# Bias rows turned on TensorE, unsummed last weights in two elements' denominators, and a piece of the MLP moved

## The chip, the cores and the metric

The kernel runs on one core of a Trainium2 chip. The metric is the device time of one execution, in microseconds; the kernel before takes 3774.46 us (median of three runs, 3773.48 to 3776.23). Lines L… are those of the kernel before unless the text says otherwise. Engines: PE is TensorE (matrix products), PEld its weight loads, DVE VectorE, ACT ScalarE, POOL GpSimd, SP the engine that issues most transfers. All data are 32-bit floats; in the trace each fp32 product shows as two passes (two MATMUL records).

## The reference

Sixteen batch elements, each an image of 256 channels by 1024 positions, go through two layers:

```python
# layer 0, per element; xs is (1024 positions, 256 channels)
qkv = (xs @ w_proj + b_proj)                 # 4 heads of 64, q k v each
attn = softmax(q @ k.T * 64 ** -0.5)
x = (attn @ v) @ w_out + b_out + xs
# layer 1
x = x + attention(group_norm(x, gn1_w, gn1_b), qkv_w, proj_w, proj_b, phys_bias)
#       8 heads of 32; phys_bias is one number per head, added before the softmax
h = group_norm(x, gn2_w, gn2_b)              # 32 groups
x = x + mlp_w2 @ gelu(mlp_w1 @ h + mlp_b1) + mlp_b2      # 256 -> 1024 -> 256
```

## The kernel before, in words

**Stages.** Each element passes attention 0 (`attention_a`, names ending in `_a`), group norm g, attention 1 (`attention_b`, names in `_b`), group norm h and the MLP (`m`). The query positions are handled in two blocks of 512 (index t), the channels in two halves of 128 (index c or co). The MLP of one element and the q, k, v products of the next fill TensorE while attention 1 waits for exponentials. Element 0 has no MLP before it, and element 15 no products after it, so these two have less to fill with.

**Attention.** Scores are computed with keys on the partitions: for each item (t, c) and each block of 128 keys, small TensorE products write scores to PSUM banks (L336, L468), ScalarE takes the exponential into an `e` tile (L344, L483), TensorE multiplies by v into an accumulator (L357, L519), and VectorE adds the `e` tiles up (L369, L498). In attention 1 a unit is two key blocks: block 0 and block 1, each with two `e` tiles of 128x1024. The function `add` is called for block 0 before the product with v of the unit before it, and for block 1 after it. The accumulator is one bank, 0, and is emptied after each unit, first by a copy on ScalarE (L530) and then by additions on VectorE (L532); the next score products use the same bank. At the end of an item the denominators are taken from the sums by products with `eones` (L541; four heads, one in each quarter of 32 columns of the array) into bank 1, copied out by ScalarE (L315), sent through DRAM to be spread over the partitions, inverted and multiplied in (L566). Small products use part of the array: "64*64" or "32*64" or "128*32" in the profile is rows by columns of one tile, and tiles on different parts run side by side.

**Tiles that change.** A setting `cols` decides whether `product` (L276 to L279) issues a 128-column product whole or as four of 32 columns. It is 32 or D inside the attentions and 128 at their ends. The function `out_proj` looks at the same setting to decide whether its two halves go to separate banks and are emptied one after the other (`apart`). At the end of attention 0, `first_half` of query block 0 (`o`, L429 to L434) runs with `cols` at 128, with the denominators `den_a` (L388) between its two halves.

**Start.** The weights `wp` arrive in six transfers from two queues (L92). The q and k copies out of PSUM add the bias `bqk` (L715), which `load_rest` fetches by six transfers of single 4-byte elements, four on ScalarE's queue behind `pb` (L143) and two on SP's (L145). `eones`, made from `pb` (L168 to L170), waits for ScalarE's exponential.

**End.** In the last element, five pieces of element 14's MLP are run inside attention 1 (`outputs[:5]`, L925) and the rest after it, where group norm h otherwise has TensorE wait; there `keep_warm` issues products whose results nobody uses. The kernel also keeps sums of denominators and of their inverses, and at its end checks that they lie in range (L959 to L970: sums, one turn on TensorE named `ok_row`, a minimum, a copy); a register is loaded from the result (L188), and a branch (L189) skips a second, general computation. These checks are written last in the program but stand between the warm products in the order of the engines, at 3708. The order within each engine's queue is set by a scheduler, with the order of the program as its start; lines inside `keep_in_program_order` are held.

Of the kernel before, what the change touches and what calls it, by code (L numbers as in the profile page):

```python
# [14 lines left out]
P = 128  # L15
# [38 lines left out]
@with_exitstack  # L54
def kernel(
    ctx: ExitStack,
    tc: tile.TileContext,
    x: bass.AP,
    w_proj: bass.AP,
    b_proj: bass.AP,  # L60
    w_out: bass.AP,
    b_out: bass.AP,
    gn1_w: bass.AP,
    gn1_b: bass.AP,
    gn2_w: bass.AP,
    gn2_b: bass.AP,
    qkv_wT: bass.AP,
    proj_wT: bass.AP,
    proj_b: bass.AP,
    phys_bias: bass.AP,  # L70
    mlp_w1T: bass.AP,
    mlp_b1: bass.AP,
    mlp_w2T: bass.AP,
    mlp_b2: bass.AP,
    out: bass.AP,
):
    nc = tc.nc
    B, C, S = x.shape
    HID = mlp_w1T.shape[1]
    CC = C // P  # L80
    SB = S // P
    NT = S // TB
    HC = HID // P
    GSZ = C // GROUPS

    const = ctx.enter_context(tc.tile_pool(name="const", bufs=1))


    wp = const.tile([P, CC, 3, HEADS0, D0], F32, name="wp")
    for t in (1, 0, 2):  # L90
        for cc in range(CC):
            (nc.gpsimd if cc else nc.scalar).dma_start(  # L92
                wp[:, cc, t],
                w_proj[cc * P : (cc + 1) * P, :].rearrange(
                    "p (h t d) -> p t h d", t=3, d=D0
                )[:, t],
            )


    bqk = const.tile([P, 3, HEADS0 // 2], F32, name="bqk")  # L100
    pb = const.tile([P, HEADS1], F32, name="pb")

    ident = const.tile([P, P], F32, name="ident")
    make_identity(nc, ident)
    mhalf = const.tile([P, CC], F32, name="mhalf")
    nc.gpsimd.memset(mhalf, -0.5)
    ones = const.tile([P, D0], F32, name="ones")
    nc.gpsimd.memset(ones, 1.0)

    def load_vec(v, n, name):  # L110
        t = const.tile([P, n], F32, name=name)
        nc.gpsimd.dma_start(t, v.rearrange("(c p) -> p c", p=P))
        return t

    bo = load_vec(b_out, CC, "bo")
    g1w = load_vec(gn1_w, CC, "g1w")
    g1b = load_vec(gn1_b, CC, "g1b")
    g2w = load_vec(gn2_w, CC, "g2w")
    g2b = load_vec(gn2_b, CC, "g2b")
    pjb = load_vec(proj_b, CC, "pjb")  # L120
    m1b = load_vec(mlp_b1, HC, "m1b")
    m2b = load_vec(mlp_b2, CC, "m2b")

    def load_mat(w, name):
        k, n = w.shape
        t = const.tile([P, k // P, n], F32, name=name)
        weights.append((t, w.rearrange("(c p) n -> p c n", p=P)))
        return t

    weights = []  # L130
    wo = load_mat(w_out, "wo")
    wq = load_mat(qkv_wT, "wq")
    wpj = load_mat(proj_wT, "wpj")
    w1 = load_mat(mlp_w1T, "w1")
    w2 = load_mat(mlp_w2T, "w2")


    def load_rest():
        bp = b_proj.rearrange("(g i t d) -> i t d g", i=2, t=3, d=D0)
        nc.scalar.dma_start(pb, phys_bias.partition_broadcast(P))  # L140
        for t in (1, 0):
            for i in range(2):
                nc.scalar.dma_start(bqk[i * D0 : (i + 1) * D0, t, :], bp[i, t])  # L143
        for i in range(2):
            nc.sync.dma_start(bqk[i * D0 : (i + 1) * D0, 2, :], bp[i, 2])  # L145
        for t, w in weights:
            nc.sync.dma_start(t, w)


    gind = const.tile([P, P // GSZ], F32, name="gind")  # L150
    nc.vector.tensor_reduce(
        gind, ident.rearrange("p (g j) -> p g j", j=GSZ), AX.X, ALU.add
    )
    gavg = const.tile([P, P // GSZ, GSZ], F32, name="gavg")
    nc.vector.tensor_scalar(
        gavg,
        gind.unsqueeze(2).to_broadcast([P, P // GSZ, GSZ]),
        1.0 / GSZ,
        None,
        ALU.mult,  # L160
    )
    gavg = gavg.rearrange("p g j -> p (g j)")


    ebias = const.tile([P, HEADS1], F32, name="ebias")
    eones = const.tile([P, HEADS1, D1], F32, name="eones")

    def exp_bias():  # L168
        nc.scalar.activation(ebias, pb, AF.Exp)
        nc.vector.tensor_copy(eones, ebias.unsqueeze(2).to_broadcast([P, HEADS1, D1]))  # L170

    bvo = const.tile([P, CC], F32, name="bvo")

    in_range = const.tile([P, 1], I32, name="in_range")

    with ExitStack() as first:
        first_pass(
            first, tc, x, out,
            dict(
                wp=wp, bqk=bqk, pb=pb, bo=bo, g1w=g1w, g1b=g1b, g2w=g2w,  # L180
                g2b=g2b, pjb=pjb, m1b=m1b, m2b=m2b, wo=wo, wq=wq, wpj=wpj, w1=w1,
                w2=w2, ident=ident, gavg=gavg, mhalf=mhalf, ones=ones, eones=eones,
                bvo=bvo, load_rest=load_rest, exp_bias=exp_bias,
                in_range=in_range,
            ),
        )

    good = nc.values_load(in_range[0:1, 0:1], min_val=0, max_val=1)  # L188
    with tc.If(good == 0):  # L189
        with ExitStack() as again:  # L190
            general_pass(
                again, tc, x, out,
                dict(
                    wp=wp, bqk=bqk, pb=pb, bo=bo, g1w=g1w, g1b=g1b, g2w=g2w,
                    g2b=g2b, pjb=pjb, m1b=m1b, m2b=m2b, wo=wo, wq=wq, wpj=wpj, w1=w1,
                    w2=w2, ident=ident, gavg=gavg, mhalf=mhalf, b_proj=b_proj,
                ),
            )


def first_pass(ctx, tc, x, out, k):
# [120 lines left out]
    def attention_a(b, qT, kT, v, project):  # L322
# [102 lines left out]
        while pending:  # L425
            weigh(*pending.pop(0))
            if not pending:


                cols[0] = P  # L430
                first_half = project(0, res)
                first_half((0,))
                yield
                first_half((1,))  # L434
                break
            yield

# [6 lines left out]
    def attention_b(b, qT, kT, v, project):  # L444
# [41 lines left out]

        def add(i, kb, es, block):
            if kb == 0 and block == 0:  # L490
                sums[i] = [
                    work.tile([P, 2, TB], F32, tag="es", name=f"es_{key}_{i}_{n}", bufs=4)
                    for n in range(G // 2)
                ]
                return
            for n in range(G // 2):
                d = sums[i][n]
                ins = nc.vector.tensor_add(d, es[n] if kb == 0 else d, es[2 * block + n])  # L498
                if block:
                    tc.keep_in_program_order(ins)  # L500
# [35 lines left out]
        def normalise(i, r, last):  # L536
            t, c = items[i]
            at_end = last and b == B - 1
            den = bank(f"den_{key}_{i}", 1)
            for g in range(G):  # L540
                nc.tensor.matmul(  # L541
                    den[g * D : (g + 1) * D, :],
                    k["eones"][:, c * G + g],
                    sums[i][g // 2][:, g % 2, :],
                    start=True,
                    stop=True,
                )
            if at_end:

                full = work.tile([P, CC * TB], F32, tag="full", name="rd_end", bufs=1)  # L550
                nc.vector.reciprocal(full[:, :TB], den)
                scale(i, r, last, full[:, :TB])
                for tot, what in ((dsum, den), (isum, full[:, :TB])):
                    part = small.tile([P, 1], F32, tag="part", name="part")
                    nc.vector.tensor_reduce(part, what, AX.X, ALU.add)
                    nc.gpsimd.tensor_add(tot[:, :1], tot[:, :1], part)
                return
            denominators(
                f"{key}_{i}", den_copy(f"{key}_{i}", den), TB,
                (3, 5) if last else (1, 1),  # L560
                lambda full: scale(i, r, last, full),
            )
# [32 lines left out]
    def out_proj(key, w, src, bias, xs, t, stats, then):  # L595
        todo = list(range(CC))

        def issue(cos=range(CC)):
            apart = cols[0] == P
            if not apart:  # L600
                both = wide(f"{key}_{t}")
            ps = {}
# [193 lines left out]
    def mlp(b, xb, hn):  # L796
# [16 lines left out]
        def reduce(t, co, half):  # L813
# [11 lines left out]
            nc.vector.scalar_tensor_tensor(  # L825
                y, ps, k["m2b"][:, co : co + 1], y, ALU.add, ALU.add
            )
            if half:
                nc.sync.dma_start(
                    out[b, co * P : (co + 1) * P, t * TB : (t + 1) * TB],  # L830
                    xb[:, co, t * TB : (t + 1) * TB],
                )

        return (
            [lambda t=t, hc=hc: hidden(t, hc) for t in range(NT) for hc in range(HC)],
# [29 lines left out]
    keep_warm(nothing, 3)  # L865
    xs = {0: load_x(0)}
    k["load_rest"]()
    tiles0, (first_qk, first_v) = qkv_0(0, xs[0])

    run_pieces(first_qk[::2] + first_qk[1::2] + first_v)  # L870
    k["exp_bias"]()


# [16 lines left out]
    for b in range(B):  # L890
# [31 lines left out]
            first = []  # L922
        if b == B - 1:

            now, end = outputs[:5], outputs[5:]  # L925
        if not first:

            fill = {m: [piece] for m, piece in enumerate(own[:5:2] + own[1::2] + own[6:])}
# [328 lines left out]
```

## Time and profile before

| what | us |
|---|---|
| median time | 3774.46 |
| profiled span | 3772.0 |
| TensorE busy | 3757.8 |
| VectorE busy | 2231.3 |
| ScalarE busy | 2034.8 |
| adds to `es_b` (L498), in all | 899.9 + 150.6 |
| one add to `es_b` (128x1024) | 1.22 |
| emptying `acc_b` on VectorE (L532), one | 0.683 |
| one exponential of 128x1024 (L483) | 0.98 |
| warm products start, first product `qk_a` | 1.47, 6.75 |
| last output addition (L825) ends | 3767.28 |

In the groups of the page, "mean ns" is the time of one instruction and "idle before" the idle time of its engine ahead of the group, with what ended most of it. Busy times of neighbours on TensorE overlap, because its instructions are pipelined; differences of start times tell what a group takes. In a row of the timeline the columns are start, length from first start to last end, engine, line, operation, output and inputs, tile and shape, count, and in brackets the idle time before with what ended it. In a row of the windows the columns are the stretch, its length, and busy time with instruction count of PE, PEld, DVE, ACT and POOL, then the granted clock as a share of full speed, the DMA share and GB/s.

### The profile page before, as it was taken

How to read it: one execution, taken by the hardware profiler on the slowest of the kernel's cores; microseconds unless marked ns; L12 is line 12 of the kernel's file. 1: busy time of each engine (PE TensorE's matmuls, PEld its weight loads, DVE VectorE, ACT ScalarE, POOL GpSimd, SP SyncE). 2: the span in 40 equal slices, each digit the busy share in tenths (PEclk: the TensorE clock that was granted, in tenths of full speed). 3: DMA queues.
4: the chain of work that ended last, by engine and by line, in shares of the span. 5: the costliest groups of instructions: out<-in, count | busy, mean ns of one | idle time of the engine just before them, and what ended most of it. 6: DMA issues, size and time to landing. Idle time of an engine off the chain costs nothing.

```text
span 3772.0 us, 86793 instructions
## 1 busy us (share of the span) xinstructions
PE 3757.8 (100%) x38335; PEld 1492.0 (40%) x38335; DVE 2231.3 (59%) x2764; ACT 2034.8 (54%) x2624; POOL 78.5 (2%) x245
## 2 busy tenths in 40 slices
PE   9999999999999999999999999999999999999999
PEld 3334343343433434334343333443334333343335
DVE  4674656656566565665656656565565655646573
ACT  4665546555465554555555455554655546555461
POOL 1000000000000000000000000000000000000000
PEclk9999999999999999999999999999999999999999
DMA  2000000000001000000000000010010100000000
GB/s 85 13 13 13 30 13 16 27 13 30 12 17 32 7 30 13 19 29 9 28 13 23 26 10 33 7 33 15 13 30 7 33 15 13 30 7 22 15 12 22
DMA packets 63052, 78.27 MB, mean 21 GB/s; under 512 B 35820, under 2 KB 37356, under 8 KB 62668
## 3 DMA queue, kind: packets, MB, share of 16 engines
q1 hardware_dynamic: 59964, 71.85, 6.2%
q8 instruction: 302, 4.95, 0.5%
q0 software_dynamic: 400, 0.41, 0.1%
q14 instruction: 82, 0.67, 0.1%
q10 hardware_dynamic: 2304, 0.40, 0.1%
HBM read 54.28 MB, written 17.56 MB: 19 GB/s over the span
## 4 chain that ended last, share of the span: by engine, by line
PE 97%; DVE 1%; issue 1%; ACT 1%; DMA 0%; ACTq 0%; POOLq 0%; POOL 0%; DVEq 0%
PE s_b L468 13%; PE acc_b L519 12%; PE m L802 12%; PE m L279 12%; PE s_a L336 12%; PE acc_a L357 11%; PE qk_b L279 6%; PE qk_a L279 6%; PE o L279 3%; PE v_b L279 3%; PE v_a L279 3%; PE j L279 3%; PE den_b L541 1%; PE den_a L388 1%; DVE es_a L369 0%
## 5 line engine op out<-in xcount | busy, mean ns | idle before, releaser
L483 ACT ACTIVATE e_b<-s_b 128x1024 f32<-128x1024 f32 (+1 forms) x1280 | 982.6, 864 | 471.0 <-PE s_b L468 471.0
L498 DVE TENSOR_TENSOR es_b<-es_b,e_b 128x1024 f32<-128x1024 f32 x768 | 899.9, 1220 | 337.5 <-ACT e_b L483 337.5
L344 ACT ACTIVATE e_a<-s_a 128x1024 f32<-128x1024 f32 x512 | 521.4, 1025 | 359.6 <-PE s_a L336 349.2
L468 PE MATMUL s_b<-q,k 32*64 32x512 f32 x8192 | 535.8, 601 | 4.0 <-DVE res_b L532 3.3
L336 PE MATMUL s_a<-q,k 64*64 64x512 f32 x4096 | 532.6, 593 | 1.1
L357 PE MATMUL acc_a<-e_a,v 64*64 64x512 f32 x4096 | 528.5, 589 | 0.0
L369 DVE TENSOR_TENSOR es_a<-es_a,e_a 128x1024 f32<-128x1024 f32 x384 | 469.3, 1222 | 85.4 <-ACT e_a L344 73.3
L519 PE MATMUL acc_b<-e_b,v 128*32 128x512 f32 x4096 | 492.1, 598 | 0.0
L279 PE MATMUL m<-g,w 128*32 128x256 f32 (+1 forms) x7664 | 464.1, 379 | 0.0
L802 PE MATMUL m<-gn_h,w 128*128 128x512 f32 x1024 | 451.3, 595 | 0.3 <-DVE gn_h L692 0.3
L810 ACT ACTIVATE g<-m,m1b 128x512 f32<-128x512 f32 x256 | 176.0, 687 | 358.2 <-PE m L802 358.2
L279 PEld LDWEIGHTS m<-g,w 128*32 128x32 f32 (+1 forms) x7664 | 276.7, 112 | 216.8 <-issue 41.9
L468 PEld LDWEIGHTS s_b<-q,k 32*64 32x64 f32 x8192 | 174.2, 130 | 288.8 <-issue 147.1
L802 PEld LDWEIGHTS m<-gn_h,w 128*128 128x128 f32 x1024 | 192.2, 190 | 230.6 <-issue 229.8
L357 PEld LDWEIGHTS acc_a<-e_a,v 64*64 64x64 f32 x4096 | 161.9, 133 | 277.5 <-issue 236.1
L336 PEld LDWEIGHTS s_a<-q,k 64*64 64x64 f32 x4096 | 152.6, 133 | 278.1 <-issue 211.7
L519 PEld LDWEIGHTS acc_b<-e_b,v 128*32 128x32 f32 x4096 | 108.5, 109 | 351.1 <-ACT e_b L483 194.7
L532 DVE TENSOR_TENSOR res_b<-res_b,acc_b 128x512 f32<-128x512 f32 x192 | 131.1, 683 | 196.2 <-PE acc_b L519 196.2
L279 PE MATMUL qk_b<-gn_g,wq 128*32 128x512 f32 (+1 forms) x1280 | 234.0, 592 | 0.0
L279 PE MATMUL qk_a<-x,wp 128*32 128x512 f32 (+1 forms) x1856 | 231.3, 592 | 2.1 <-ACT q L715 1.5
L736 DVE TENSOR_TENSOR v<-v_b,eones 128x512 f32<-128x512 f32 x64 | 44.0, 688 | 291.2 <-PE v_b L279 291.2
L498 DVE TENSOR_TENSOR es_b<-e_b,e_b 128x1024 f32<-128x1024 f32 x128 | 150.6, 1218 | 0.0
(121 smaller groups left out, 2096.3 us busy)
## 6 DMA issues: line engine op xcount, KB each, us to landing
rd_a<-row_a SPq DMA_DIRECT2D x64, 256.0 KB
out_dram<-x SPq DMA_DIRECT2D x64, 256.0 KB
rd_b<-row_b SPq DMA_DIRECT2D x252, 64.0 KB
x<-in_x_dram SPq DMA_DIRECT2D x30, 512.0 KB
w<-in_L_conv_mlp_w_dram SPq DMA_DIRECT2D x2, 1024.0 KB
x<-in_x_dram SPq DMA_DIRECT2D x4, 256.0 KB
sp_b<-d_b SPq DMA_DIRECT2D x63, 8.0 KB
row_b<-inv_b SPq DMA_DIRECT2D x63, 8.0 KB
```

Source lines behind the costliest of these rows:

```text
L279: nc.tensor.matmul(o[sl], w[:, sl], r, **flags)
L336: nc.tensor.matmul(s[h : h + HALF, g, :], kT[g * D : (g + 1) * D, c, kb * P + h : kb * P + h + HALF], qT[g * D : (g + 1) * D, c, t * TB : ...
L344: nc.scalar.activation(e, s, AF.Exp, scale=float(D) ** -0.5)
L357: nc.tensor.matmul(accs[i][h][g * D : (g + 1) * D, :], v[h * HALF : (h + 1) * HALF, kb, c * 2 + g], e[h * HALF : (h + 1) * HALF, g, :], st ...
L369: nc.vector.tensor_add(sums[i], held[i] if kb == 1 else sums[i], e)
L468: nc.tensor.matmul(outs[g][h : h + HALF, :], kT[g * D : (g + 1) * D, c, k0 : k0 + HALF], qT[g * D : (g + 1) * D, c, t * TB : (t + 1) * TB] ...
L483: nc.scalar.activation(to, s, AF.Exp, scale=float(D) ** -0.5)
L498: ins = nc.vector.tensor_add(d, es[n] if kb == 0 else d, es[2 * block + n])
L519: nc.tensor.matmul(acc[g * D : (g + 1) * D, :], v[:, kb + m, c * G + g], es[2 * m + g // 2][:, g % 2, :], start=(m == 0), stop=(m == 1),)
L532: nc.vector.tensor_add(r, r, acc)
L802: nc.tensor.matmul(ps, k["w1"][:, cc, hc * P : (hc + 1) * P], hn[0][:, cc, t * TB : (t + 1) * TB], start=(cc == 0), stop=(cc == CC - 1),)
L810: nc.scalar.activation(g, ps, AF.Gelu, bias=k["m1b"][:, hc : hc + 1])
```

## The change

Five things change.

1. The bias columns are loaded as six rows of 128 (`brow`, three transfers in pieces of 256 bytes, behind the first weight transfer on ScalarE's queue), turned on TensorE by one transpose and copied to `bqk` by VectorE. It is meant to have the biases early without transfers of single elements.
2. The first half of `o` is issued while `cols` is still 32, with its halves still in separate banks, so that TensorE doesn't change its tiles around it.
3. In elements 0 and 15 (`spared`), the `e` tiles of an item's last unit aren't added to the sums. The denominators are taken from the sums and from these tiles, three products for each head instead of one, accumulated in PSUM. It is meant to relieve VectorE.
4. In the last element four pieces instead of five run in the attention, so that one more is there for the end. With it, the scheduler puts `ok_row` behind the last product of the kernel.
5. The last output tile is sent in two halves, each after its own addition.

```diff
+    brow = const.tile([3 * HEADS0 // 2, P], F32, name="brow")
     for t in (1, 0, 2):
+        if t == 0:
+            bp = b_proj.rearrange("(g i t d) -> t g i d", i=2, t=3, d=D0)
+            for u in range(3):
+                nc.scalar.dma_start(
+                    brow[u * 2 : (u + 1) * 2].rearrange("g (i d) -> g i d", d=D0), bp[u]
+                )
         for cc in range(CC):
...
     def load_rest():
-        bp = b_proj.rearrange("(g i t d) -> i t d g", i=2, t=3, d=D0)
         nc.scalar.dma_start(pb, phys_bias.partition_broadcast(P))
-        for t in (1, 0):
-            for i in range(2):
-                nc.scalar.dma_start(bqk[i * D0 : (i + 1) * D0, t, :], bp[i, t])
-        for i in range(2):
-            nc.sync.dma_start(bqk[i * D0 : (i + 1) * D0, 2, :], bp[i, 2])
...
-                cols[0] = P
-                first_half = project(0, res)
-                first_half((0,))
-                yield
-                first_half((1,))
+                first_half = project(0, res)
+                first_half((0,), True)
+                yield
+                first_half((1,), True)
+                cols[0] = P
                 break
...
+        spared, apart = b in (0, B - 1), {}
+
         def add(i, kb, es, block):
...
+            if spared and kb == SB - 2:
+                apart[i] = es
+                return
...
             for g in range(G):
-                nc.tensor.matmul(
-                    den[g * D : (g + 1) * D, :],
-                    k["eones"][:, c * G + g],
-                    sums[i][g // 2][:, g % 2, :],
-                    start=True,
-                    stop=True,
-                )
+                parts = [sums[i][g // 2]]
+                if i in apart:
+                    parts += apart[i][g // 2 :: 2]
+                for m, part in enumerate(parts):
+                    nc.tensor.matmul(
+                        den[g * D : (g + 1) * D, :],
+                        k["eones"][:, c * G + g],
+                        part[:, g % 2, :],
+                        start=(m == 0),
+                        stop=(m == len(parts) - 1),
+                    )
...
-        def issue(cos=range(CC)):
-            apart = cols[0] == P
+        def issue(cos=range(CC), apart=False):
+            apart = apart or cols[0] == P
...
-            if half:
-                nc.sync.dma_start(
-                    out[b, co * P : (co + 1) * P, t * TB : (t + 1) * TB],
-                    xb[:, co, t * TB : (t + 1) * TB],
-                )
+            each = b == B - 1 and (t, co) == (NT - 1, CC - 1)
+            if half or each:
+                sl = slice(t * TB + (half * n if each else 0), t * TB + (half + 1) * n)
+                nc.sync.dma_start(out[b, co * P : (co + 1) * P, sl], xb[:, co, sl])
...
     k["load_rest"]()
+    ps, n = bank("bqk", 0), k["brow"].shape[0]
+    turn = nc.tensor.transpose(ps[:, :n], k["brow"], k["ident"][:n, :n])
+    nc.vector.tensor_copy(k["bqk"].rearrange("p t g -> p (t g)"), ps[:, :n])
     tiles0, (first_qk, first_v) = qkv_0(0, xs[0])
 
-    run_pieces(first_qk[::2] + first_qk[1::2] + first_v)
+    start = first_qk[::2] + first_qk[1::2] + first_v
+    start[0]()
+    with tc.issue_after(turn.ins):
+        start[1]()
+    run_pieces(start[2:])
...
-            now, end = outputs[:5], outputs[5:]
+            now, end = outputs[:4], outputs[4:]
```

More of the change, by code (lines that the diff above doesn't have):

```diff
@@ L182 @@
                 w2=w2, ident=ident, gavg=gavg, mhalf=mhalf, ones=ones, eones=eones,
-                bvo=bvo, load_rest=load_rest, exp_bias=exp_bias,
+                bvo=bvo, brow=brow, load_rest=load_rest, exp_bias=exp_bias,
                 in_range=in_range,
```

## The prediction, made before the changed kernel was timed

> **What bounds the kernel now.** I read the shares of the engines and the chain that ended last, then the timeline of each stretch that the change touches.
>
> ```profile
> PE 3757.8 (100%) x38335; PEld 1492.0 (40%) x38335; DVE 2231.3 (59%) x2764; ACT 2034.8 (54%) x2624; POOL 78.5 (2%) x245
> ...
> PE 97%; DVE 1%; issue 1%; ACT 1%; DMA 0%; ACTq 0%; POOLq 0%; POOL 0%; DVEq 0%
> ```
>
> TensorE is the bound: a microsecond added to its work costs one, and work taken from VectorE counts only where TensorE waits for it. The granted clock is 1.00. A 512-column pass takes 0.43 us and an fp32 product makes two passes; small tiles run side by side.
>
> ```profile
> 13.02 1.98 PE L279 MATMUL qk_a<-x,wp 128*128 128x512 f32 x4 [0.61 <-ACT k L715]
> 16.50 3.70 PE L279 MATMUL qk_a<-x,wp 128*128 128x512 f32 x8 [1.50 <-ACT q L715]
> ...
> 15.76 0.69 ACT L715 ACTIVATE q<-qk_a,bqk 128x512 f32<-128x512 f32 x1 [2.80 <-DMA bqk<-in_L_conv_b_proj_dram]
> ```
>
> The start stalls twice: the q copy waits for the bias loads, and TensorE for the copy.
>
> ```profile
> 85.19 2.75 PE L357 MATMUL acc_a<-e_a,v 64*64 64x512 f32 x24
> 87.87 1.98 PE L279 MATMUL o<-res_a,wo 128*128 128x512 f32 x4
> 89.79 1.07 PE L388 MATMUL den_a<-es_a,ones 128*32 128x256 f32 x16
> 90.79 1.98 PE L279 MATMUL o<-res_a,wo 128*128 128x512 f32 x4
> 92.61 10.46 PE L279 MATMUL qk_a<-x,wp 128*128 128x512 f32 x24
> ```
>
> Starts, not busy times, show the cost: 87.87 to 89.79 is 1.92 us for four passes worth 1.72. Changing between 64- or 32-wide and whole tiles costs something each time.
>
> ```profile
> 189.65 1.92 PE L519 MATMUL acc_b<-e_b,v 128*32 128x512 f32 x16
> 191.51 1.07 PE L468 MATMUL s_b<-q,k 32*64 32x512 f32 x2
> 193.49 1.97 PE L468 MATMUL s_b<-q,k 32*64 32x512 f32 x30 [0.92 <-DVE res_b L532]
> 195.39 1.92 PE L519 MATMUL acc_b<-e_b,v 128*32 128x512 f32 x16
> 197.13 1.04 PE L541 MATMUL den_b<-es_b,eones 128*32 128x512 f32 x8
> 198.12 2.82 PE L468 MATMUL s_b<-q,k 32*64 32x512 f32 x32
> ```
>
> This is attention 1 of element 0, without MLP work to fill. Its 32 score passes fit eight abreast into four slots, 1.72 us, but take 195.39 − 191.51 = 3.88: TensorE waits for VectorE to empty a bank (L532). The denominators' 8 passes, four abreast, take about two slots (197.13 to 198.12).
>
> ```profile
> 190.49 2.35 DVE L498 TENSOR_TENSOR es_b<-es_b,e_b 128x1024 f32<-128x1024 f32 x2
> ...
> 192.76 0.68 DVE L532 TENSOR_TENSOR res_b<-res_b,acc_b 128x512 f32<-128x512 f32 x1
> ...
> 198.29 0.63 ACT L315 COPY d_b<-den_b 128x512 f32<-128x512 f32 x1
> ```
>
> The emptying stands behind two adds to sums; after the denominators a copy on ScalarE is waited for.
>
> **What the Trainium skill says.** "TensorEngine Tiling (Array Packing)", key properties: changing the tiling mode drains TensorE. The trace agrees: 64*64 to 128*128 costs 0.11 us in the median, 128*32 to 128*128 0.11 and 0.10 more at the second pass. "TensorE: Matmul & The Clock Gate", Part 3: a 64-deep window pulls weight loads ahead, while matmuls start strictly in program order. The trace departs from this: each tile's two passes are neighbours in the program, yet all eight tiles of a score group make their first pass, 7 ns apart (155.534 to 155.581), before any second pass. So TensorE does run past a tile that is occupied; how far isn't shown. "DMA: Bandwidth & Descriptors": pieces under 512 bytes miss the line rate, and about 2 us are fixed; the 4-byte pieces of the bias columns landed at 15.66, issued from 4.82 on. "Runtime: NRT & Kernel Launch", instruction fetch: a taken branch out of the window waits for a fetch; here VectorE branches at 3767.435 and shows its next event 3.44 us later.
>
> **The change part by part.**
>
> *Start.* Six column loads, each 0.62 to 0.75 us of issuing, become three row loads behind the first weight load; a turn on TensorE and a copy on VectorE follow. That copy stands behind `eones`, which waits for `pb`, table load and `ebias`. Before, `pb` was issued by 3.45 and had landed by 10.2; its issue now comes later, behind the rows. The table load (1.28), which had to wait till 10.88 for ScalarE to issue the columns, can run ahead of `pb`. An estimate from these: `pb` at 10, `ebias` 10.2, `eones`, `gind`, `gavg` (0.29, 0.28, 0.23) till 10.9, bias ready at 11.05, first k copy (0.68) till 11.8. The fourth group of products could start at 11.81 but starts at 13.02 with a slot lengthened to a loss of 0.78 in all; the next wait loses 1.67. Both go, less 0.15 for the turn: **−2.3**. Bounds: 0, if `pb` comes late, and −2.44.
>
> *Output projection.* Its first half of the last query block is cut into 32-column tiles in all 16 elements: acc_a, o, den_a, o lost 0.11 + 0.20 + 0.14 + 0.10 = 0.55 over their passes. The later `j`, already cut so, takes 3.43 us for 32 passes four abreast, its ideal 3.44, so the cut itself is free. Left are a change before o, none before den_a, and 0.21 before the whole half: 0.34. Gain 0.21 × 16 = **−3.3** (bounds −1.5 and −4).
>
> *Denominators.* In elements 0 and 15 each of the 8 items drops four adds of about 1.22 us on VectorE, and its denominators take 12 products (24 passes) instead of 4. Four abreast that is six slots of 0.43 instead of two: 4 × 0.43 = 1.72 on TensorE, which has no other work then; × 8 = **+13.7**. The program now gives one tile three products in a row before the next tile; abreast they run only if TensorE looks past the five passes that wait. That is the disputed cost: no more than 1.72 if it does; if one tile must take up all but its last pass before the next begins, the 24 passes take up to 22 slots, 9.4 us, or 8.6 extra. I take the low end, since the trace shows running past seven tiles' second passes with their loads (some 28 instructions; now some 36 are needed). What the dropped adds give back: only the emptying that stands behind block 0 of the last unit's adds comes earlier. At 191.51 the product ended about 191.5; the emptying could begin at 191.7 instead of 192.76: 1.0. The like place at 170.25 gains 0.8 (171.28 to 170.5); element 15 has MLP pieces between and gains about 0.7; sum **−2.6** (bounds −1 and −5). The waits after the denominators stay, since they hang on the copy at 198.29; those at 186.25 and 207.73 stand behind adds of earlier units, which remain. The final e tiles are held until the denominators end, about 199.8; the next unit's exponentials that reuse them need scores from 199.8 on anyway: nothing.
>
> *The piece kept for the end.* An MLP piece of 3.45 us moves from the attention into the stretch between gm_h (3707.04) and the hidden products (3711.41), where TensorE mostly runs warm-up products. About 1.4 of those 4.4 us are taken by it, but `rstd` then stands behind its addition (0.48): **−1.0** (bounds 0 and −1.4). In the attention nothing opens: the reciprocal of the last denominators (3.36) is still covered.
>
> *End.* The check of the range (`ok_row`) now comes after the last product instead of at 3708.15, so its minimum and copy follow the last addition (3767.28), then the register load (about 0.5) and VectorE's branch with its 3.44 us. Branch now at 3767.435, then about 0.9 later; the last output's DMA, to about 3770.7, hid it nearly to the end. Halving that DMA saves up to 0.35. **+0.8** (bounds −0.35 and +1.2).
>
> Sum: −2.3 − 3.3 + 13.7 − 2.6 − 1.0 + 0.8 = +5.3, so 3774.5 + 5.3 = **3780**. All low bounds together give +0.5, all high ones (den look-ahead apart) +12.
>
> **The rivals.**
>
> *TensorE doesn't look far enough.* For: nothing in the trace has more than two passes in a row on one tile. Against: it does pass eight occupied tiles. With room for four passes a tile, tiles begin 4 passes apart: 3 × 1.72 + 2.58 = 7.74 instead of 2.58 us, 5.16 × 8 = 41 more, **3821**; the worst case above, 55 more, 3835. A window that falls only a few instructions short costs one or two slots an item, 3783 to 3787.
>
> *VectorE was the bound of these stages.* For: of 112 us it is busy 90 in either element (third busy time of the first two rows), against 59 in the steady stretch of the last row.
>
> ```profile
> 124.00:236.00 112.00, 108.99 (x1161) 33.48 (x1163) 89.82 (x92) 79.36 (x105) 3.48 (x8) 1.00 0.04 11
> 3590.00:3702.00 112.00, 110.97 (x1329) 41.83 (x1314) 89.57 (x101) 68.53 (x92) 3.74 (x8) 1.00 0.05 16
> 500.00:612.00 112.00, 112.00 (x972) 44.36 (x966) 59.37 (x77) 60.24 (x82) 1.59 (x5) 1.00 0.04 11
> ```
>
> Score groups there lose 16.1 us (element 0) and 9.5 (element 15) over their passes. If the waits that name L532 go, some 16 in all, 13 more than I count, the time is **3766**: faster. Against: they come from order, one add waiting for an exponential ahead of the emptying, more than from a backlog.
>
> *No gain at the start*, as the bias copy comes late behind `eones`: **3782**.
>
> **How the numbers follow.** Forecast with its spread 0.55, VectorE's relief 0.15, too short a look-ahead 0.25 (a third of it the small form), no start gain 0.05. The range from 3763 to 3800 leaves out the serial tiles (0.17) and the best of the relief (0.03). Faster by over 0.2% (below 3767): most of the relief, 0.13. Slower (above 3782): the look-ahead, nearly a third of the forecast's own spread and part of the last rival, 0.43. Within: 0.44.
>
> **What would show it.** The copy to bqk near 11, and no wait for q after it; o in 32-wide tiles starting without a loss before den_a; den_b x24 in 2.6 us (right) or 7 to 9 (wrong); the emptying behind unit 6 a microsecond earlier; the branch on VectorE about 0.9 later after the last x. A mistake in the den passes outweighs all the others.

## The result and the profile after

The changed kernel takes 3801.7 us (median of four runs, 3801.28 to 3801.94) against 3774.5: a ratio of 1.0071, 95% interval 1.0054 to 1.0089. It is 27 us slower, where the prediction said 5 slower with a range up to 3800. Lines below are those of the changed kernel, 2 to 20 higher than before (L470 scores, L528 product with v, L541 emptying, L554 denominators, L838 last addition); in the experiments they can differ by a few.

First the engines' busy times, and the shares of the chain that ended last, in the page of the changed kernel:

```profile
PE 3787.9 (100%) x38800; PEld 1497.6 (39%) x38800; DVE 2195.7 (58%) x2733; ACT 2038.7 (54%) x2624; POOL 79.4 (2%) x245
...
PE 98%; DVE 1%; issue 1%; ACT 1%; POOL 0%; DVEq 0%
```

VectorE did lose 36 us of work. TensorE, which bounds the kernel, gained 30 us. The timeline of TensorE at the start and at the end of an attention 0, as shown of before:

```profile
6.73 3.60 PE L281 MATMUL qk_a<-x,wp 128*128 128x512 f32 x8
10.26 0.22 PE L882 MATMUL bqk<-ident,brow 6*128 6x6 f32 x1
10.41 10.57 PE L281 MATMUL qk_a<-x,wp 128*128 128x512 f32 x24
...
83.82 1.47 PE L359 MATMUL acc_a<-e_a,v 64*64 64x512 f32 x12
85.21 1.92 PE L281 MATMUL o<-res_a,wo 128*32 128x512 f32 x16
86.95 1.05 PE L390 MATMUL den_a<-es_a,ones 128*32 128x256 f32 x16
87.82 1.90 PE L281 MATMUL o<-res_a,wo 128*32 128x512 f32 x16
89.65 10.57 PE L281 MATMUL qk_a<-x,wp 128*128 128x512 f32 x24
```

Both waits of the start are gone, and 85.21 to 86.95 is 1.74 us for an ideal of 1.72. These parts did as forecast. The loss is in the next view, one item's denominators in element 0:

```profile
176.35 1.02 PE L554 MATMUL den_b<-es_b,eones 128*32 128x512 f32 x2
177.21 0.59 PE L554 MATMUL den_b<-e_b,eones 128*32 128x512 f32 x1
177.22 0.62 PE L554 MATMUL den_b<-es_b,eones 128*32 128x512 f32 x1
177.64 0.59 PE L554 MATMUL den_b<-e_b,eones 128*32 128x512 f32 x1
177.67 0.59 PE L554 MATMUL den_b<-es_b,eones 128*32 128x512 f32 x1
178.07 0.62 PE L554 MATMUL den_b<-e_b,eones 128*32 128x512 f32 x2
178.10 0.62 PE L554 MATMUL den_b<-es_b,eones 128*32 128x512 f32 x1
...
179.84 1.91 PE L554 MATMUL den_b<-e_b,eones 128*32 128x512 f32 x6
181.68 2.71 PE L470 MATMUL s_b<-q,k 32*64 32x512 f32 x32
```

The inputs tell a tile's products apart: `es_b` is its first, `e_b` its second and third, and each product is two passes. At 176.35 the first tile works alone. Only at 177.22, when it has begun its second product (177.21), does the second tile begin its first; the third follows at 178.10. Each tile begins two passes after the one before it, so 24 passes take 3 × 2 + 6 = 12 slots instead of 6: 181.68 − 176.35 = 5.33 us, where it was 0.99.

The whole difference by stages, from the starts of the same groups in the two traces (spans 3799.5 and 3772.0): first denominators of attention 0 at 60.02 instead of 62.68, −2.66; in each of the 16 elements −0.17 to −0.18 at `o`, −2.9 in all; attention 1 of element 0 **+15.3**; of element 15, up to gm_h, +13.6 although the piece of 3.45 us has left it, so **+17.0** for what stayed; gm_h to the hidden products 7.33 instead of 4.37, +2.96; last addition to the end 6.02 instead of 4.75, +1.3. They add up to 27.5.

### The profile page after: what moved, and what is told of

Read it like the earlier page. It is cut to its first block, busy times and chain, and to the rows that moved or that the text cites. A ratio compares the mean times of both kernels' runs of the same rounds, so it can differ in the third digit from the quotient of the medians.

```text
span 3799.5 us, 87656 instructions
## 1 busy us (share of the span) xinstructions
PE 3787.9 (100%) x38800; PEld 1497.6 (39%) x38800; DVE 2195.7 (58%) x2733; ACT 2038.7 (54%) x2624; POOL 79.4 (2%) x245
## 4 chain that ended last, share of the span: by engine, by line
PE 98%; DVE 1%; issue 1%; ACT 1%; POOL 0%; DVEq 0%
PE s_b L470 13%; PE acc_b L528 12%; PE m L815 12%; PE m L281 12%; PE s_a L338 12%; PE acc_a L359 11%; PE qk_b L281 6%; PE qk_a L281 6%; PE v_b L281 3%; PE o L281 3%; PE v_a L281 3%; PE j L281 3%; PE den_b L554 2%; PE den_a L390 1%; DVE es_a L371 0%
## 5 line engine op out<-in xcount | busy, mean ns | idle before, releaser
L507 DVE TENSOR_TENSOR es_b<-es_b,e_b 128x1024 f32<-128x1024 f32 x736 | 862.5, 1221 | 363.1 <-ACT e_b L485 363.1
L470 PE MATMUL s_b<-q,k 32*64 32x512 f32 x8192 | 534.9, 601 | 2.5 <-DVE res_b L541 1.7
L528 PE MATMUL acc_b<-e_b,v 128*32 128x512 f32 x4096 | 492.1, 598 | 0.0
L470 PEld LDWEIGHTS s_b<-q,k 32*64 32x64 f32 x8192 | 174.3, 130 | 286.2 <-issue 151.3
L541 DVE TENSOR_TENSOR res_b<-res_b,acc_b 128x512 f32<-128x512 f32 x192 | 131.2, 684 | 216.6 <-PE acc_b L528 216.6
L528 PEld LDWEIGHTS acc_b<-e_b,v 128*32 128x32 f32 x4096 | 108.5, 109 | 351.5 <-ACT e_b L485 194.7
```

What stands on the lines that cost most here:

```text
L470: nc.tensor.matmul(outs[g][h : h + HALF, :], kT[g * D : (g + 1) * D, c, k0 : k0 + HALF], qT[g * D : (g + 1) * D, c, t * TB : (t + 1) * TB] ...
L528: nc.tensor.matmul(acc[g * D : (g + 1) * D, :], v[:, kb + m, c * G + g], es[2 * m + g // 2][:, g % 2, :], start=(m == 0), stop=(m == 1),)
L541: nc.vector.tensor_add(r, r, acc)
```

## The experiments

Kernels timed together share runs of the kernel before on the same chip: 3773.96 us for e1 to e4, 3774.24 for e5 to e8, 3774.09 for e9 and e10. The changed kernel's 3801.70 stands beside 3774.51, so differences to it are good to about half a microsecond. Ratios are to the kernel before, with a 95% interval in brackets.

**e1, the products in another order.**

```diff
-            for g in range(G):
...
-                for m, part in enumerate(parts):
+            for m, g in [(m, g) for m in range(n_parts) for g in range(G)]:
```

> The changed kernel, with the 12 denominator products of an item in another order: the first product of all four column tiles, then the second of all four, then the third. Theory A (program order: a tile's six passes in a row hold the next tile back, which is why an item's denominators take 5.33 us in the changed kernel): the 24 passes run four abreast in 2.6 to 2.7 us, 8 items gain about 2.7 us each, time about 3780. Theory B (the order is innocent: accumulating three products, or reading the e tiles, is what takes the time): still 5.3 us an item, time about 3802.

Measured: 3780.31 us, ratio 1.0016 (1.0010 to 1.0023). The timeline of TensorE in this kernel, the same item:

```profile
174.63 1.04 PE L553 MATMUL den_b<-es_b,eones 128*32 128x512 f32 x8
175.49 1.90 PE L553 MATMUL den_b<-e_b,eones 128*32 128x512 f32 x16
177.32 1.93 PE L470 MATMUL s_b<-q,k 32*64 32x512 f32 x20
```

All 24 passes take 2.69 us: four abreast, as the prediction had counted. The same products in another order save 21.4 us by the medians, so theory A stands: neither the accumulation nor the inputs cost it, but the order.

**e2, nothing spared.**

```diff
-        spared, apart = b in (0, B - 1), {}
+        spared, apart = False, {}
```

> The changed kernel with every last unit added to the sums again (nothing spared), so the denominators are 8 passes as before. Theory A (the denominators cost 4.34 us an item, 34.7 in all, against 2.4 gained back from VectorE): 3801.7 - 34.7 + 2.4 = about 3769.4, 5 us under the kernel before. Rival (VectorE's relief is worth 10 us or more, so that more than the denominators has to be wrong elsewhere): about 3777 to 3780.

Measured: 3770.02 us, ratio 0.9988 (0.9982 to 0.9995): faster than before. The denominators are back at 0.99 us an item. Between e1 and e2 lies the sparing at its best order: it costs 10.3 us by the medians, near the 13.7 − 2.6 of the prediction. In neither order does the relief of VectorE pay for the passes.

**e3, half of it spared.**

```diff
-            if spared and kb == SB - 2:
-                apart[i] = es
+            if spared and kb == SB - 2 and block:
+                apart[i] = es[2:]
```

> The changed kernel, with only block 1 of the last unit spared (two adds an item instead of four) and two products a tile (16 passes), still tile by tile. Theory Q (each tile can have about five of its own instructions waiting, which two products don't exceed): the four tiles run abreast, 1.7 us an item, time about 3769.4 + 8 x 0.86 = 3776, less up to 1 for the adds. Theory W (about six waiting instructions in all tiles together): the third tile starts one slot late and the fourth two, 2.6 us an item, about 3783. Theory O (a tile always starts two passes after the one before it): ten slots, 4.3 us, about 3797.

Measured: 3775.87 us, ratio 1.0004 (0.9995 to 1.0012). TensorE in this kernel, still tile by tile in the program:

```profile
173.62 1.08 PE L554 MATMUL den_b<-es_b,eones 128*32 128x512 f32 x8
174.48 1.08 PE L554 MATMUL den_b<-e_b,eones 128*32 128x512 f32 x8
175.49 2.75 PE L470 MATMUL s_b<-q,k 32*64 32x512 f32 x32
```

16 passes in 1.87 us, abreast. Theories W and O fall: four passes in a row on a tile don't hold the next tile back.

**e4, by pairs of tiles,** an edit on e1:

```diff
-            for m, g in [(m, g) for m in range(n_parts) for g in range(G)]:
+            for m, g in [(m, g) for g0 in (0, 2) for m in range(n_parts) for g in (g0, g0 + 1)]:
```

> The changed kernel with its 12 products ordered by pairs of tiles: first, second, third product of tiles 0 and 1 in turn, then of tiles 2 and 3. Theory Q (about five waiting instructions for each tile): the second pair starts two passes after the first, 8 slots, 3.4 us an item, time about 3788. Theory W (about six waiting instructions in all): the second pair starts three passes after the first, 9 slots, 3.9 us, about 3791. A third way (only two tiles are ever under way when each has several products): 12 slots, 5.2 us, about 3801.

Measured: 3787.29 us, ratio 1.0034 (1.0022 to 1.0046).

```profile
175.36 1.03 PE L553 MATMUL den_b<-es_b,eones 128*32 128x512 f32 x4
176.22 0.60 PE L553 MATMUL den_b<-e_b,eones 128*32 128x512 f32 x2
176.23 0.62 PE L553 MATMUL den_b<-es_b,eones 128*32 128x512 f32 x2
...
177.08 1.92 PE L553 MATMUL den_b<-e_b,eones 128*32 128x512 f32 x12
178.93 1.50 PE L470 MATMUL s_b<-q,k 32*64 32x512 f32 x12
```

Two tiles start together, and the other two start two passes later (176.23), when the first two begin their second product: 3.57 us. Two tiles with six passes each hold the next ones back no longer than one such tile did, so the limit is one for each tile, as theory Q has it. The changed kernel's own trace agrees: when its third tile starts (178.10), four passes wait in the two tiles ahead, one in the first and three in the second; at 176.78 four passes were waiting too, all of the first tile, and the second tile was held.

**e5, the range check early.** Nothing spared, and the check stands in the program ahead of the last MLP:

```diff
     later.flush()
+    ok = small.tile([P, 2], F32, name="ok", bufs=1)
...
     run_pieces(hidden + outputs)
-    ok = small.tile([P, 2], F32, name="ok", bufs=1)
...
```

> The changed kernel with nothing spared and with the range check (ok_row, least, in_range) written ahead of the last MLP, so that it stands behind the warm products instead of behind the last product of the kernel. Theory A (the late check costs the end: from the last addition to the end 6.0 to 6.3 us instead of 4.7): about 4.7 us from the last addition to the end, time about 1.4 under the nothing-spared kernel, 3768.6. Rival (the two half transfers of the last tile are what lengthens the end): still 6.0 or more, 3770.

Measured: 3769.14 us, ratio 0.9985 (0.9978 to 0.9992). From the last addition to the end 4.57 us instead of the 6.24 of e2, so the late check did cost the end. VectorE's branch comes 0.15 us after the last addition instead of 1.20. In e2 TensorE, too, branches only then (3763.23), and its next event (3767.40) comes 0.85 after VectorE's and ends last; in e5 it has branched at 3758.97, ahead of the last addition. The time itself is only 0.9 below e2, within the scatter of both: in its profile the start gained 1.46 us, in that of e2 2.36 (see e9).

**e6, five pieces in the attention again,** on top of e5:

```diff
-            now, end = outputs[:4], outputs[4:]
+            now, end = outputs[:5], outputs[5:]
```

> As e5, with five pieces in the attention of the last element again, as in the kernel before. Theory A (keeping the fourth piece for the end is worth 3.45 - 2.96 = 0.5 us, what the changed kernel's profile shows): 0.5 slower than e5, 3769.1. Rival (a fifth piece in the attention fills a wait there, and keeping it back gains nothing or loses): the same as e5 or faster.

Measured: 3768.89 us, ratio 0.9984 (0.9977 to 0.9991); the same as e5. In e5 the attention of element 15 (from its last denominators in attention 0 to gm_h) is 2.98 us shorter than in e6, not 3.45, and the stretch from gm_h to the last MLP 2.96 longer: nothing is left. The missing 0.46 is at the last `j` product of e5, which now waits for the reciprocal of the denominators. Theory A fails where nothing is spared; five pieces together with sparing were not run.

**e7, one transfer for the last tile,** on top of e5:

```diff
-            each = b == B - 1 and (t, co) == (NT - 1, CC - 1)
+            each = False
```

> As e5, with the last output tile sent in one transfer as before. Theory A (the halved transfer saves 0 to 0.35 us at the end, since the branch, not the transfer, comes last): 3768.6 to 3769.0, and 4.7 us from the last addition to the end. Rival (the two transfers cost): faster than e5.

Measured: 3768.98 us, ratio 0.9984 (0.9977 to 0.9991), 4.73 us from the last addition to the end, against 4.57 in e5, 4.20 in e6 and 5.03 in e9 with the halved transfer. Neither side shows: splitting the transfer is worth nothing that stands out of the scatter. The traces of e5, e6 and e7 show why: the last packet of the output ends 0.4 to 1.2 us before VectorE's first event after its branch, so the transfer, whole or halved, is hidden, as theory A had it.

**e8, the bias rows alone** in the kernel before (parts of the diff around `brow`, `turn` and `start`).

> The kernel before, with the bias rows and their turn alone. Theory A (both waits at the start go, 2.66 us by the changed kernel's first denominators): first denominators 2.7 earlier, time about 3771.3. Rival (what the start gains is given back, since the weights for the next stages come later): first denominators 2.7 earlier but the end 1 us or less.

Measured: 3772.02 us, ratio 0.9992 (0.9984 to 1.0001): some 2 us gained by the medians, at the edge of what the interval can tell. The profiled execution was the longest of its 13 (3774.78), and shows how the gain can be lost. ScalarE, VectorE and TensorE in that profile, and a row of the windows:

```profile
12.33 0.21 ACT L171 ACTIVATE ebias<-pb 128x8 f32<-128x8 f32 x1 [5.06 <-DMA pb<-in_L_conv_phys_bias_dram]
...
12.98 0.15 DVE L872 COPY bqk<-bqk 128x6 f32<-128x6 f32 x1
...
13.91 4.54 PE L281 MATMUL qk_a<-x,wp 128*128 128x512 f32 x6 [2.50 <-ACT k L717]
...
15.00:18.00 3.00, 3.00 (x5) 1.35 (x4) 0.00 (x0) 0.70 (x2) 0.00 (x0) 0.50 1.02 368
```

Here `pb` landed at 12.3 instead of 10.2, and the copy of the bias, which TensorE had turned at 9.3, stood behind it until 12.98. TensorE waited 2.5 us for it, and lost more behind the wait: from 15.08 to 17.64 its passes started 0.85 us apart instead of 0.43, which is about 1.7 us; the granted clock from 15 to 18 us was 0.50. In the kernel before, whose waits at the start are 0.61 and 1.50 us, the clock in the windows after them stays at 1.00. So nothing was gained in this execution (first denominators 0.82 later than before), although its first product had started 1.16 us earlier (5.59 instead of 6.75). Neither theory describes it whole: there is a gain by the medians, and in this profile it was lost to one late transfer.

**e9, the bias copy freed of `pb`,** on top of e6:

```diff
-    k["exp_bias"]()
+    with tc.issue_after(k["last_qk"].ins):
+        k["exp_bias"]()
```

> As e6 (nothing spared, early check, five pieces), with ebias and eones queued behind the first q and k copies, so that the copy of the turned bias doesn't stand behind pb any more. Theory A (how much the start gains is set by when pb lands, 10.2 to 12.3 us in the profiles: the bias copy waits for it behind eones and ebias): the copy comes within 0.4 us of the turn, no wait in the first q and k products, first denominators 2.7 to 3.8 us earlier than in the kernel before, time about 0.5 to 1 under e6, 3768.2. Rival (the rows themselves or the weights of q set it): the same wait as in e6 and no gain.

Measured: 3767.70 us, ratio 0.9981 (0.9974 to 0.9989), the lowest median of all here. VectorE and ScalarE in its profile:

```profile
9.94 0.17 DVE L883 COPY bqk<-bqk 128x6 f32<-128x6 f32 x1 [4.49 <-PE bqk L882]
...
10.14 0.69 ACT L728 ACTIVATE k<-qk_a,bqk 128x512 f32<-128x512 f32 x1 [2.86 <-DVE bqk L883]
```

The copy follows its turn (9.68) by 0.26 us, and the first denominators are 3.24 us earlier than before; in the seven profiles of e1 to e7, which start as the changed kernel does, 1.46 to 2.73. Part of these differences is the start of the first product, which varies from 5.55 to 6.75 us. Counted from it, the first denominators follow after 53.29 us in e9 and in the changed kernel, where the copy comes 0.26 and 0.57 us behind the turn; after 53.57 to 54.47 in e1 to e7, with 0.68 to 2.01; after 57.91 in e8, with 3.70; and after 55.93 in the kernel before. So theory A holds for the mechanism, and the rest of e9's gain is its earlier first product (6.15). The medians of e9 and e6 are too close for their intervals to tell them apart.

**e10, `o` alone** in the kernel before (the two hunks around `first_half` and `apart`).

> The kernel before, with the first half of o in 32-column tiles alone. Theory A (each element gains 0.17 us, as the distance of the denominators from element to element shows in the changed kernel): 16 x 0.17 = 2.8 us, about 3771.5. The prediction said 0.21 an element, 3.3 in all, 3771. Rival (what is gained there is lost in the products that follow): no change.

Measured: 3770.71 us, ratio 0.9991 (0.9982 to 0.9999). From the first to the last element its denominators of attention 0 move 2.9 us closer, 0.17 to 0.18 an element, so theory A stands; 0.9 more in its profile lies ahead of the first denominators, where nothing was changed: the first product starts 0.34 earlier, and the waits at the start are shorter. By the medians e8 gains 2.2 and e10 3.4 us; e6, which has both and the split transfer, gains 5.4.

## Why the prediction was wrong, by its own steps

**Denominators: wrong, and this is nearly the whole miss,** 21 of 22 us. The step that failed is "I take the low end, since the trace shows running past seven tiles' second passes with their loads". It counted how many instructions TensorE had passed over in all, some 28 against 36 needed. Both counts take in passes that had begun: what really waited was half of the 28, and would be 30 of the 36, so the step was a long one. And the runs showed that what counts is how many of them belong to one tile. In the trace of before no tile had more than one pass waiting ahead of another tile's first. In the changed kernel the first tile has five; at its second pass (176.78), with four left waiting, the next tile is still held; at its third (177.209), with three left, the next begins its weight load 5 ns later (177.214). e3, with three passes waiting, runs abreast, and e4 shows the limit to be each tile's own. The term measured 4.34 us an item, 34.7 in all, instead of 1.72 and 13.7.

The rival "TensorE doesn't look far enough" had the mechanism, and its "room for four passes a tile", counted with the pass under way, is what the runs showed. Its sum was wrong: of six passes such room leaves two to be worked off before the next tile begins, not four. With two, an item is 12 slots or 5.16 us and the time 3780 + 8 × 2.58, about 3801, where it said 3821. (Its worst case, by its own condition, is 3 × 5 + 6 = 21 slots and not 22.) A chance of 0.25 for it, with 0.17 for the serial tiles left outside the range, was too little: nothing in the trace bore on that case, and the bound from above was known.

**What the dropped adds give back: right.** Predicted −2.6 (its parts, 1.0, 0.8 and 0.7, make 2.5). The group that took 3.88 us before, in the changed kernel:

```profile
194.59 1.92 PE L528 MATMUL acc_b<-e_b,v 128*32 128x512 f32 x16
196.44 2.85 PE L470 MATMUL s_b<-q,k 32*64 32x512 f32 x32
199.22 1.06 PE L528 MATMUL acc_b<-e_b,v 128*32 128x512 f32 x8
```

199.22 − 196.44 = 2.78: 1.1 gained, with 1.0 predicted; 0.9 at the other place, with 0.8 predicted. Over element 0 it is 4 × 4.34 − 15.26 = 2.1, over element 15 4 × 4.34 − 17.03 = 0.3, so 2.4. Against e2 it is 34.7 − 31.7 = 3.0, since e2 pays 0.46 at its last `j` (see e6). By the first sum element 15 gave less than the 0.7 predicted. The rival that VectorE bounded these stages falls: VectorE lost 16 adds of 1.22 us there in element 0, 19.5 us of work, and TensorE's waits only 2.1.

**Start: right on average.** −2.66 in the profile against −2.3, and −2.2 in the mean of the eight profiles that start this way (the changed kernel and e1 to e7). The order of the estimate (`pb` at 10, bias ready at 11.05, k copy till 11.8) matches 10.19, 10.98 and a first k copy from 11.02. Its bound of 0 "if `pb` comes late" was too narrow: in the profile of e8 `pb` did come late, and the first denominators came 0.82 later than before. The lower clock behind a long wait was not counted.

**Output projection: right in kind,** 0.17 to 0.18 an element against 0.21. From the first `o` to the q and k products it takes 4.44 us (85.21 to 89.65) instead of 4.74, 0.30 less; but the change to whole tiles now falls to those products, whose 24 passes take 10.40 us instead of 10.30 (89.65 to 100.05, 92.61 to 102.91). −2.9 over all against −3.3.

**Piece for the end: half.** −0.5 (2.96 − 3.45) against −1.0. The −0.5 takes the piece at its 3.45 us. In the stretch after gm_h eight warm products still run ahead of the piece (3730.43 to 3731.40), 1.0 us that the profile shows and the estimate doesn't count. "In the attention nothing opens" held in the changed kernel and in e1: VectorE's statistics and the last emptying, which stand ahead of the last reciprocal, are done 1.7 us after the denominators begin, and 24 passes outlast them. In e2 the 8 passes take 0.97 us, and the reciprocal starts 1.2 us after their end (3685.86 against 3684.65), behind that emptying. So a wait opens where nothing is spared, and e5 against e6 shows that the gain is nought.

**End: right in kind,** +1.3 against +0.8, just above its bound of 1.2. VectorE's branch came 1.03 later behind the last addition, with 0.9 predicted, and the time from the branch to its next event was 3.67 us instead of 3.44; over all profiles it varies from 2.9 to 3.7. The end of the chain in the changed kernel:

```profile
3793.01 0.48 DVE x L838
3793.49 0.20 DVE least L989
3793.69 0.02 issue
3793.72 0.14 DVE in_range L990
```

Minimum and copy follow the last addition, and the load and the branch follow them. What e5 took back by moving the check ahead is this term. That TensorE, ScalarE and GpSimd branch only behind the late check too, and that one of them can end last (TensorE in e2), the prediction left out.

With the measured terms: −2.7 − 2.9 + 34.7 − 2.4 − 0.5 + 1.3 = +27.5, as measured between the spans.

## What to carry to other kernels

Where several products accumulate into each of several small tiles, write the loop over the tiles inside and the loop over the products outside: the same 24 passes took 2.7 us in that order and 5.3 in the other. Work taken from an engine that isn't the bound is worth only the waits whose last releaser it is: 36 us fewer on VectorE brought 2.4 to 3.0, and the passes that paid for it were on the engine that was. And when a trace shows that an engine gets past something, ask whether it shows it for the case at hand; if not, the range has to reach the other bound.

## What the runs showed of the hardware

On TensorE with four tiles of 128*32, in fp32, one tile can have three passes waiting (four in a row, e3) without holding back the next tile's instructions, and can't have four (at 176.78 in the changed kernel). Two of the three still had their weights to load, in e3 and in the changed kernel at 177.21, where the next tile is let in. Whether the limit is one of instructions, of passes or of products, the runs don't tell. The Trainium skill ("TensorE: Matmul & The Clock Gate", Part 3) speaks of one window of 64 and of matmuls that start in program order; here the 12 instructions of one tile were enough to stop the next, while passes of different tiles did start out of that order (in e3 the first pass of the second tile starts at 173.630, ahead of the first tile's second at 174.053).

In the profile of e8 a wait of 2.5 us on TensorE was followed by a granted clock of 0.50 from 15 to 18 us; after the wait of 1.50 us in the kernel before it stayed at 1.00. Where between the two the change lies, and whether the wait alone brings it, the runs don't tell.
